# Gated cross-attention with a mixture of experts on one core: another turn table, and two small products split into quadrants of 32 rows

## The chip, the cores and the metric

The kernel runs on one core of a Trainium2 chip. A core has a matrix engine (TensorE, in the profile PE, with its weight loads as PEld), a vector engine (VectorE, DVE), a scalar engine (ScalarE, ACT), a general engine (GpSimd, POOL) and a queue engine (SyncE, SP), each with its own instruction stream in program order, and 16 DMA engines. The metric is device time in microseconds for one execution; less is better.

## The reference, cut to what matters

64 batches of 128 tokens with 128 features, a context of 77 tokens a batch, 16 heads of 8, and 8 experts of which each token takes 2. All float32.

```python
x = x + tanh(g_xattn) * attention(layernorm(x), ctx, mask)     # 16 heads, 77 keys, then Wo
n = layernorm(x)
gate = softmax(n @ Wg)                     # 8 experts
topk_scores, topk_idx = top_k(gate, 2)
topk_scores /= topk_scores.sum(-1) + 1e-8
fused = (n @ W11) * sigmoid(n @ W11) * (n @ W12)    # per expert, inner width 256
x = x + tanh(g_ffn) * sum_k topk_scores[k] * (fused @ W2)[topk_idx[k]]
```

The kernel computes each token only for the two experts that it takes: rows are scattered to the region of their expert in DRAM, worked off in tiles of 128 rows, and scattered back.

## The kernel before, in words

**Groups and turns.** Four batches are a group, so there are 16 groups of 512 tokens. The attention runs in 64 turns, one for each batch. In turn i, PE computes the score products of batch i (`scores`, L865), transposes the scores of batch i-1 (`turn`, L887), mixes values for batch i-2 (`mix`, L919, 24 short products of 32 columns for each of two halves), makes the value blocks of batch i+2 (`values`, L838 and L850, 12 very short products) and transposes what is left of i-1 (`turn_last`, L900). DVE takes maxima of the scores and subtracts them (L874, L877), ACT takes exponentials. The scores have one PSUM buffer, so a turn's scores wait for the subtraction of the turn before.

**The turn table.** All else is done by groups, in steps. The table `AT` gives each step a turn, counted from the group's first, and PRE or POST, before or after that turn's own work. Group g does step s in turn 4g + AT[s]. So in any turn steps of several groups meet, and four turns are a period in which one group's worth of each step is done. Within one place steps run by group number. A POST step of a turn is issued just before a PRE step of the next. The order on PE, ACT, DVE and POOL is the program's order; SP's is planned.

**The steps that the change touches.** Loads (`loads`), statistics, shift and rows of the first layernorm (`stats_a*`, `shift_a`, `rows_a*`), the context's masks on POOL (`sel_0` to `sel_2`), the queries (`queries_t`, `queries`), then after the attention the quotients (`quotients`), the output product (`project`, L589), the sum (`residual`, L595), and the second layernorm (`stats_f*`, `shift_f`, `rows_t`). Then comes the routing: `logits` (four products of a batch's 128 tokens with the gate weights, 8 columns, L642), `less_max`, `gates_exp`, `gates` and `experts` on DVE (two best of eight, L661 to L685), `counts` on POOL (running counts of each expert, L693 and L697), `places` (two products, L705 and L708: how many rows stand ahead of each token), `places_in` on DVE (the row in DRAM, L713 to L722), and eight scatters a group, `dispatch00` to `dispatch31` (batch, choice): each a memset and an indirect DMA on POOL (L726, L727).

**Two parts.** Groups 0 to 11 are part 0, groups 12 to 15 part 1. When the last group of a part has been counted, `tiles_count`, `tiles_ends`, `tiles_list`, `tiles_turn` and `tiles_keep` make the part's list of tiles, and `bounds0` to `bounds3` have SP write padding behind each expert's rows. In other groups these steps are empty.

**The second half.** After the turns, 142 tiles go through PE (`turned` L1034, `up` L1044, `flip` L1059, `down` L1067), ACT and DVE, and POOL scatters each result (L1075, L1076). Steps of the last groups that had no turn left (`rest`) are dealt out one a tile, in the table's order, during part 0's tiles. A part's row loads (L1030) wait for all of its scatters and paddings. At the end the results are fetched, added and stored.

**PSUM.** All products but scores and values take one of three slots in a ring (`product`); a product waits for the readers of the one three before it.

Of the kernel before, what the change touches and what calls it, by code (L numbers as in the profile page):

```python
# [21 lines left out]
G = 4  # L22
# [3 lines left out]
PRE, POST = 0, 1  # L26
# [11 lines left out]
def tile_gated_xattn_moe(  # L38
# [17 lines left out]
    nc = tc.nc  # L56
    B, S, D = x.shape
    M, CD = context.shape[1:]
    E, _, I = W11.shape
    P = 128  # L60
# [26 lines left out]
    def part_of(g):  # L87
        return parts[g >= SPLIT]
# [22 lines left out]
    gates = const.tile([P, 2], F32, name="gates")  # L111
# [4 lines left out]
    wg = wts.tile([D, E], F32, name="wg")  # L116
# [12 lines left out]
    def load_expert(k):  # L129
# [48 lines left out]
    earlier = const.tile([P, P], F32, name="earlier")  # L178
    nc.gpsimd.memset(earlier, 1.0)
    nc.gpsimd.affine_select(  # L180
        earlier, earlier, pattern=[[1, P]], compare_op=ALU.is_gt, fill=0.0,
        base=0, channel_multiplier=-1,
    )
    ones = const.tile([P, P], F32, name="ones")
# [32 lines left out]
    for q in range(NQ):  # L217
        for k in range(2):
            r = 32 * q + 16 * k
# [89 lines left out]
    with ExitStack() as ph:  # L309
# [77 lines left out]
        def product(shape, n):  # L387
            return ring[0].tile(shape, F32, tag="pr", name=n)

        def transposed(src, n):  # L390
# [10 lines left out]


        AT = {
            "loads": (-15, PRE),
            "stats_a0": (-14, PRE),
            "sel_0": (-14, PRE),
            "stats_a1": (-10, PRE),
            "sel_1": (-13, PRE),
            "shift_a": (-9, POST),
            "sel_2": (-11, POST),  # L410
            "context_t": (-7, POST),
            "rows_a0": (-9, POST),
            "rows_a1": (-8, PRE),
            "keys": (-4, POST),
            "queries_t": (-7, POST),
            "queries": (-5, PRE),
            "inverses": (6, PRE),
            "quotients": (6, POST),
            "project": (7, POST),
            "residual": (7, POST),  # L420
            "stats_f0": (8, POST),
            "stats_f1": (9, PRE),
            "shift_f": (10, PRE),
            "rows_f0": (10, PRE),
            "rows_f1": (11, PRE),
            "rows_f2": (11, PRE),
            "rows_t": (11, POST),
            "logits": (13, PRE),
            "less_max": (13, PRE),
            "gates_exp": (14, PRE),  # L430
            "gates": (15, PRE),
            "experts": (15, PRE),
            "counts": (15, PRE),
            "places": (17, PRE),
            "places_in": (17, PRE),
            "tiles_count": (16, PRE),
            "tiles_ends": (16, PRE),
            "tiles_list": (17, PRE),
            "tiles_turn": (17, POST),
            "tiles_keep": (18, PRE),  # L440
            "bounds0": (18, PRE),
            "bounds1": (18, PRE),
            "bounds2": (18, PRE),
            "bounds3": (20, PRE),
            "dispatch00": (17, POST),
            "dispatch01": (17, POST),
            "dispatch10": (18, PRE),
            "dispatch11": (18, POST),
            "dispatch20": (19, PRE),
            "dispatch21": (19, POST),  # L450
            "dispatch30": (19, POST),
            "dispatch31": (20, POST),
        }
        TURN = {}

# [2 lines left out]
        def step(name):  # L458
            def add(f):
                STEP[name] = f  # L460
                TURN.setdefault(AT[name], []).append(name)
                return f

            return add
# [173 lines left out]
        @step("logits")  # L638
        def logits(gr, g):
            gr.pg = product(ge, f"pg_{g}")  # L640
            for b in range(G):
                nc.tensor.matmul(  # L642
                    gr.pg[:, b, :], gr.xT[:, b * S : (b + 1) * S], wg, start=True, stop=True
                )

        @step("less_max")
        def less_max(gr, g):
# [54 lines left out]
        @step("places")  # L702
        def places(gr, g):
            gr.pp = product(ge, f"pp_{g}")
            nc.tensor.matmul(gr.pp, earlier, gr.both, start=True, stop=False)  # L705
            pt = part_of(g)
            i = (g - pt.g0) * G
            nc.tensor.matmul(gr.pp, ones, pt.run[:, i : i + G], start=False, stop=True)  # L708

        @step("places_in")  # L710
        def places_in(gr, g):
# [267 lines left out]
        for i in range(NBT + 2):  # L979
# [8 lines left out]
            if 0 <= i - 2 < NBT:  # L988
                g, b = divmod(i - 2, G)
# [143 lines left out]
        for g in range(SPLIT):  # L1133
            for j, f in enumerate((combine(0), combine(1), store)):
                k = t0 + 3 + (TOPK * g + min(j, 1)) * n1 // (TOPK * SPLIT)
# [52 lines left out]
```

## Time and profile before

| | us |
|---|---|
| median of 3 runs | 690.18 (686.12 to 691.53) |
| profiled execution: its time | 691.94 |
| its span, first to last instruction | 690.2 |
| PE busy | 622.8 |
| POOL busy | 444.5 |
| ACT busy | 438.1 |
| DVE busy | 431.4 |
| first score product, last score product | 20.1, 379.0 |
| first and last product of the tiles | 389.4, 671.3 |

The mean granted clock of TensorE is 0.957. The page gives busy times by engine and, in 40 equal slices, by time; below that stand the chain of work that ended last and the costliest groups of instructions, each with the idle time of its engine before it and what ended it ("issue": nothing that the profile shows). In tables of windows the columns are the window, its length, busy time and number of instructions of PE, PEld, DVE, ACT and POOL, the clock granted to TensorE, the DMA engines' busy share and GB/s. In a timeline they are start, duration, engine, line, operation, and in brackets the idle time before it. A float32 product is two records on PE.

### The profile page before, as it was taken

The numbers are of one execution on the slowest core, as the hardware profiler recorded it, in microseconds if no ns is written. First come the engines' busy times: TensorE is split into PE (matmuls) and PEld (weight loads), VectorE is DVE, ScalarE is ACT, GpSimd is POOL, SyncE is SP. The second block draws the span as 40 slices with busy tenths as digits, with TensorE's granted clock in tenths as the row PEclk, the third lists the DMA queues.
The fourth block names the chain that finished last, engine by engine and source line by source line (L and its number), as shares of the span: only waits on it lengthen the run. The fifth ranks groups of instructions, "written<-read, shape, count | busy, mean of one in ns | idle before, by whom it ended". The sixth has DMA issues, their size and how long they took to land.

```text
span 690.2 us, 21362 instructions
## 1 busy us (share of the span) xinstructions
PE 622.8 (90%) x7703; PEld 450.6 (65%) x7703; DVE 431.4 (63%) x1296; ACT 438.1 (63%) x1184; POOL 444.5 (64%) x771
## 2 busy tenths in 40 slices
PE   4799999999999999999997899999987999999980
PEld 3577877777777877777774666656554556556560
DVE  4758799788787878786788544443343433346642
ACT  3698888677767867786764555576463445545450
POOL 4411125576576657666376458888888888888782
PEclk9999999999989999999999899999998999999995
DMA  4493000111111100010012242232322331458825
GB/s 106 124 287 86 16 15 29 38 31 35 29 35 34 33 26 26 22 31 30 18 31 69 68 100 63 73 82 63 83 77 67 92 82 57 104 189 242 246 83 182
DMA packets 64510, 53.55 MB, mean 78 GB/s; under 512 B 14131, under 2 KB 58235, under 8 KB 64408
## 3 DMA queue, kind: packets, MB, share of 16 engines
q1 hardware_dynamic: 46952, 30.78, 17.1%
q0 software_dynamic: 8640, 17.06, 7.3%
q10 hardware_dynamic: 8816, 4.36, 2.2%
q8 instruction: 63, 1.03, 0.7%
q14 instruction: 39, 0.32, 0.2%
HBM read 28.88 MB, written 24.20 MB: 77 GB/s over the span
## 4 chain that ended last, share of the span: by engine, by line
PE 62%; POOL 14%; issue 9%; DVE 5%; ACT 5%; DMA 3%; SPq 1%; POOLq 1%; another core or an unknown queue 0%; DVEq 0%; ACTq 0%
PE po L919 12%; PE pu L1044 9%; POOL yb L1076 9%; PE tp L887 9%; PE sc L865 6%; PE pot L1067 4%; POOL spare_w L1075 3%; PE tl L900 3%; PE pq L566 2%; PE phh L1059 2%; PE py L589 2%; PE pg L642 2%; PE pv L850 2%; PE pc L528 2%; PE ptt L1034 2%
## 5 line engine op out<-in xcount | busy, mean ns | idle before, releaser
L727 POOL DMA_INDIRECT xg<-rows,dest x128 | 129.0, 1007 | 70.0 <-DVE gm L649 44.4
L1076 POOL DMA_INDIRECT yb<-y,xt x142 | 139.6, 983 | 34.7 <-issue 16.0
L1044 PE MATMUL pu<-wx,xTt 128*128 x284 | 155.1, 629 | 6.6 <-issue 5.6
L1052 DVE TENSOR_TENSOR ht<-sgt,pu 128x256 f32<-128x256 f32 x142 | 59.9, 422 | 113.8 <-ACT sgt L1050 56.9
L1050 ACT ACTIVATE sgt<-pu 128x256 f32<-128x256 f32 x142 | 54.6, 384 | 92.8 <-PE pu L1044 51.6
L874 DVE TENSOR_REDUCE mx<-sc 128x16 f32<-128x1232 f32 x64 | 91.8, 1434 | 31.8 <-PE sc L865 24.6
L1059 PEld LDWEIGHTS phh<-ident,ht 128*128 128x128 f32 x284 | 39.5, 142 | 81.5 <-issue 66.3
L892 ACT ACTIVATE pT<-tp,drop 128x512 f32<-128x512 f32 x128 | 81.3, 680 | 12.6 <-PE tp L887 11.8
L1067 PE MATMUL pot<-wx,hTt 128*128 x568 | 87.0, 276 | 0.0
L887 PEld LDWEIGHTS tp<-ident,pe 128*128 128x128 f32 x512 | 60.5, 151 | 31.5 <-issue 9.2
L877 DVE TENSOR_TENSOR pe<-sc,mx 128x1024 f32<-128x1024 f32 x64 | 78.4, 1225 | 2.2
L887 PE MATMUL tp<-ident,pe 128*128 128x128 f32 x512 | 77.3, 298 | 1.3 <-ACT kb L555 0.6
L1067 PEld LDWEIGHTS pot<-wx,hTt 128*128 128x128 f32 x568 | 75.0, 192 | 0.2 <-ACT y L1073 0.2
L1073 ACT ACTIVATE y<-pot,xt 128x128 f32<-128x128 f32 x142 | 52.6, 370 | 24.0 <-PE ptt L1034 9.1
L1036 DVE COPY xTt<-ptt 128x128 f32<-128x128 f32 x142 | 41.4, 291 | 39.0 <-PE phh L1059 14.7
L370 POOL TENSOR_TENSOR rs_a<-rs_a,live 128x4 f32<-128x4 f32 x15 | 3.0, 201 | 89.7 <-ACT rs_a L367 81.8
L865 PE MATMUL sc<-kb,qT 32*128 32x308 f32 x512 | 56.8, 512 | 3.5 <-ACT kb L555 1.8
L919 PE MATMUL po<-pT,va 128*32 128x128 f32 x1536 | 57.2, 284 | 3.0 <-issue 2.3
L919 PE MATMUL po<-pT,own 128*32 128x128 f32 x1536 | 58.6, 277 | 1.4 <-issue 1.4
L1059 PE MATMUL phh<-ident,ht 128*128 128x128 f32 x284 | 55.0, 276 | 3.4 <-ACT hTt L1061 3.2
L1061 ACT COPY hTt<-phh 128x256 f32<-128x256 f32 x142 | 52.4, 369 | 8.6 <-PE ptt L1034 6.0
L1044 PEld LDWEIGHTS pu<-wx,xTt 128*128 128x128 f32 x284 | 43.9, 195 | 17.8 <-issue 16.4
(169 smaller groups left out, 1140.9 us busy)
## 6 DMA issues: line engine op xcount, KB each, us to landing
xt<-xg SPq DMA_DIRECT2D x142, 66.0 KB
ys<-yb SPq DMA_DIRECT2D x16, 512.0 KB
x<-in_x_dram SPq DMA_DIRECT2D x15, 256.0 KB
out_dram<-x ACTq DMA_DIRECT2D x15, 256.0 KB
yb<-y,xt POOLq DMA_INDIRECT x142
wx<-in_L_ffn_W_dram SPq DMA_DIRECT2D x2, 1024.0 KB
xg<-rows,dest POOLq DMA_INDIRECT x128
xg<-empty SPq DMA_DIRECT2D x30, 66.0 KB
```

The costliest lines, as they stand in the source:

```text
L727: i = nc.gpsimd.indirect_dma_start(out=part_of(g).xg[:, :], out_offset=bass.IndirectOffsetOnAxis(ap=gr.dest[:, k, b : b + 1], axis=0), in_ ...
L865: nc.tensor.matmul(sc[:, q, :W], gr.qT[r, b * S : (b + 1) * S], gr.kb[r, b].rearrange("p h j -> p (h j)"), start=True, stop=True,)
L874: nc.vector.tensor_reduce(mx[:, :, :, 0], sv, AX.X, ALU.max)
L877: nc.vector.tensor_tensor(dst[:, :, :, : j1 - j0], sv[:, :, :, j0:j1], mx.to_broadcast([P, NQ, HQ, j1 - j0]), ALU.subtract,)
L887: nc.tensor.transpose(tp[:, u, :], pe[:, q + u // 2, 2 * (u % 2) : 2 * (u % 2) + 2].rearrange("p h j -> p (h j)"), ident,)
L892: nc.scalar.activation(pT[:, 2 * q : 2 * q + 4], tp, AF.Exp, bias=drop[:, 0, i : i + 1], scale=scale)
L919: nc.tensor.matmul(po[32 * q : 32 * q + 32, v, :], w, pT[:, 2 * q + c if c < 2 else 8 + q // 2, :], start=(c == 0), stop=(c == 2),)
L1044: nc.tensor.matmul(pu.rearrange("p j i -> p (j i)"), ti.xT, wxf[:, bass.ds(ti.e, 2 * I)], start=True, stop=True,)
L1052: nc.vector.tensor_tensor(ti.h.rearrange("p c i -> p (c i)"), sg, pu[:, 1], ALU.mult)
L1059: nc.tensor.transpose(pt[:, c], ti.h[:, c], ident)
L1067: nc.tensor.matmul(po, ti.hT[:, c], wxf[:, bass.ds(ti.e + w, D)], start=(c == 0), stop=(c == NC - 1),)
L1076: i = nc.gpsimd.indirect_dma_start(out=ti.pt.yb[:, :], out_offset=bass.IndirectOffsetOnAxis(ap=ti.x[:, D : D + 1].bitcast(I32), axis=0), i ...
```

## The change

The table `AT` gets other turns. Most of the routing comes sooner by a half to two turns: the gates' exponential, `gates`, `experts`, `places` (from before turn 17 to after turn 15), the tile list and seven of eight scatters by more than one turn. `quotients`, `project` and `residual` come one turn later, `queries_t` one sooner, `bounds3` two later. And `logits` and `places` are split: in place of one product with 128 rows of result there are four with 32 rows each, which take 32 columns of the stationary operand each. `logits` has 16 products instead of 4, `places` 8 instead of 2. Nothing else changes.

```diff
-            "loads": (-15, PRE),
+            "loads": (-16, POST),
             "stats_a0": (-14, PRE),
             "sel_0": (-14, PRE),
             "stats_a1": (-10, PRE),
-            "sel_1": (-13, PRE),
-            "shift_a": (-9, POST),
-            "sel_2": (-11, POST),
+            "sel_1": (-11, POST),
+            "shift_a": (-10, POST),
+            "sel_2": (-10, POST),
             "context_t": (-7, POST),
-            "rows_a0": (-9, POST),
+            "rows_a0": (-8, PRE),
             "rows_a1": (-8, PRE),
             "keys": (-4, POST),
-            "queries_t": (-7, POST),
+            "queries_t": (-8, POST),
             "queries": (-5, PRE),
             "inverses": (6, PRE),
-            "quotients": (6, POST),
-            "project": (7, POST),
-            "residual": (7, POST),
+            "quotients": (7, POST),
+            "project": (8, POST),
+            "residual": (8, POST),
             "stats_f0": (8, POST),
             "stats_f1": (9, PRE),
-            "shift_f": (10, PRE),
+            "shift_f": (9, POST),
...
-            "rows_t": (11, POST),
+            "rows_t": (12, PRE),
             "logits": (13, PRE),
             "less_max": (13, PRE),
-            "gates_exp": (14, PRE),
-            "gates": (15, PRE),
-            "experts": (15, PRE),
+            "gates_exp": (13, PRE),
+            "gates": (14, POST),
+            "experts": (14, POST),
             "counts": (15, PRE),
-            "places": (17, PRE),
-            "places_in": (17, PRE),
-            "tiles_count": (16, PRE),
-            "tiles_ends": (16, PRE),
-            "tiles_list": (17, PRE),
-            "tiles_turn": (17, POST),
-            "tiles_keep": (18, PRE),
-            "bounds0": (18, PRE),
-            "bounds1": (18, PRE),
-            "bounds2": (18, PRE),
-            "bounds3": (20, PRE),
-            "dispatch00": (17, POST),
-            "dispatch01": (17, POST),
-            "dispatch10": (18, PRE),
-            "dispatch11": (18, POST),
-            "dispatch20": (19, PRE),
-            "dispatch21": (19, POST),
-            "dispatch30": (19, POST),
-            "dispatch31": (20, POST),
+            "places": (15, POST),
+            "places_in": (15, POST),
+            "tiles_count": (15, POST),
+            "tiles_ends": (15, POST),
+            "tiles_list": (16, PRE),
+            "tiles_turn": (16, POST),
+            "tiles_keep": (16, POST),
+            "bounds0": (15, POST),
+            "bounds1": (17, POST),
+            "bounds2": (17, POST),
+            "bounds3": (22, PRE),
+            "dispatch00": (15, POST),
+            "dispatch01": (16, PRE),
+            "dispatch10": (16, POST),
+            "dispatch11": (16, POST),
+            "dispatch20": (16, POST),
+            "dispatch21": (16, POST),
+            "dispatch30": (18, PRE),
+            "dispatch31": (19, POST),
...
             for b in range(G):
-                nc.tensor.matmul(
-                    gr.pg[:, b, :], gr.xT[:, b * S : (b + 1) * S], wg, start=True, stop=True
-                )
+                for r in range(0, P, 32):
+                    nc.tensor.matmul(
+                        gr.pg[r : r + 32, b, :], gr.xT[:, b * S + r : b * S + r + 32], wg,
+                        start=True, stop=True,
+                    )
...
             gr.pp = product(ge, f"pp_{g}")
-            nc.tensor.matmul(gr.pp, earlier, gr.both, start=True, stop=False)
             pt = part_of(g)
             i = (g - pt.g0) * G
-            nc.tensor.matmul(gr.pp, ones, pt.run[:, i : i + G], start=False, stop=True)
+            for k, (w, of) in enumerate(((earlier, gr.both), (ones, pt.run[:, i : i + G]))):
+                for r in range(0, P, 32):
+                    nc.tensor.matmul(
+                        gr.pp[r : r + 32], w[:, r : r + 32], of, start=(k == 0), stop=(k == 1)
+                    )
```

## The prediction

> **What bounds the kernel now.** I read the page first: which engine is full, and where. PE is busy 90% of the span and the chain that ended last lies on it for 62%.
>
> ```profile
> PE 622.8 (90%) x7703; PEld 450.6 (65%) x7703; DVE 431.4 (63%) x1296; ACT 438.1 (63%) x1184; POOL 444.5 (64%) x771
> ...
> PEclk9999999999989999999999899999998999999995
> ```
>
> The clock row has dents at slices 12, 23 and 31; it rounds shorter ones away. The table of windows, cut at starts of score products four turns (one period, one group of batches) apart or a multiple of it, shows them all.
>
> ```profile
> 129.03:226.49 97.46, 92.86 (x1602) 73.83 (x1601) 76.72 (x232) 71.78 (x189) 61.49 (x112) 0.91 0.12 33
> 226.49:248.73 22.24, 21.36 (x402) 17.11 (x401) 19.04 (x58) 17.71 (x48) 15.39 (x28) 1.00 0.11 33
> 248.73:297.82 49.09, 47.08 (x801) 37.46 (x800) 38.34 (x116) 35.94 (x95) 30.75 (x56) 0.90 0.08 25
> ```
>
> The first row is four periods (24.4 us each, clock 0.91), the last two (24.5, 0.90), the middle one period at full clock (22.2). Same work: a period that meets the half clock is 2.2 us longer, and there are six such periods (and one more dent at 320 us). PE is busy 94 to 96% of these rows, so PE sets the pace. Where the half clock comes from:
>
> ```profile
> 241.72:245.36 3.64, 3.58 (x76) 2.77 (x75) 3.50 (x5) 2.73 (x6) 3.14 (x6) 1.00 0.11 37
> 245.36:248.78 3.42, 2.71 (x33) 2.41 (x33) 1.66 (x9) 2.35 (x8) 0.98 (x2) 1.00 0.08 25
> 248.78:252.19 3.41, 3.41 (x23) 2.24 (x26) 3.16 (x9) 1.85 (x6) 2.66 (x4) 0.50 0.07 22
> ```
>
> A 3.4 us window with 33 PE products instead of some 80 is followed by 3.4 us at 0.50. Two things thin that window. One: `values` (L838, L850) is a burst of 24 short products, and where it meets a scatter (L727 on POOL) it halts.
>
> ```profile
> 239.69 0.30 PE L838 MATMUL pv<-wv,cT 96*32 96x64 f32 x8
> 239.80 0.29 PE L850 MATMUL pv<-wv,czs 96*32 96x16 f32 x16
> ...
> 253.02 1.00 POOL L727 DMA_INDIRECT xg<-rows,dest  x1 [0.16 <-issue]
> ...
> 253.51 0.33 PE L850 MATMUL pv<-wv,czs 96*32 96x16 f32 x10
> ...
> 254.31 0.29 PE L850 MATMUL pv<-wv,czs 96*32 96x16 f32 x6 [0.47 <-issue]
> ```
>
> Undisturbed the burst runs through; under a scatter it stops for 0.47 us with nothing awaited. In the timeline of 125 to 300 us this happens about twice (1.1 us) in the turn before `logits` and once (0.5 us) in the one after, nearly every period. Two: right behind come `places` and `logits`, which move 32 and 8 columns.
>
> ```profile
> L642 PE MATMUL pg<-wg,xT_f 128*128 128x8 f32 x128 | 17.3, 262 | 0.0
> L642 PEld LDWEIGHTS pg<-wg,xT_f 128*128 128x128 f32 x128 | 16.3, 198 | 0.2
> ...
> L708 PE MATMUL pp<-run,ones 128*128 128x32 f32 x32 | 6.2, 276 | 0.0
> L705 PEld LDWEIGHTS pp<-both,earlier 128*128 128x128 f32 x32 | 5.7, 190 | 1.5
> ```
>
> `logits` is 8 records in 1.0 us, 0.125 us each: the pace of 128-column weight loads. `places` is 4 in 0.63 us.
>
> **Part 1: the quadrants.** `logits` becomes 32 records of 32 columns, `places` 16. Nearest row: the burst above, 24 records in 0.42 us, 17.5 ns each (the L919 products: 24 in 0.57 to 0.68). So 32 x 17.5 = 0.56 us for 1.0, and 16 x 17.5 = 0.28 for 0.63: 0.79 us a group. Against it stands the Trainium skill: "TensorE: Matmul & The Clock Gate", section LDWEIGHTS, prices a load by its columns at P/1.2 ns, so four quarters cost what the whole cost: 32 x 27 = 0.85, 16 x 27 = 0.43, saving 0.35; and "TensorEngine Tiling", Key Properties, says that a change of tiling mode drains the engine. The trace contradicts the load price (17.5 ns) and prices the drain: weight loads idle 0.17 us at the step from the 128-column transposes to L919. Two switches more a group, some 0.3 us, is the charge. Saving: 0.79 less 0.3, about 0.5; ends 0 and 0.8. PE takes 28 instructions more each for loads and products; if bursts of them meet scatters, that is rival C.
>
> **Part 2: the table.** A step at (k, POST) stands beside one at (k+1, PRE); call that boundary k+1. By boundary, modulo 4: PE had transposed rows and `project` at 0, keys, `places`, `logits` at 1, context and query transposes at 2, queries at 3. Now: `places` and transposed rows at 0 (before 1.6 us, now 0.35 + 0.5); `project` (1.06), keys (0.5), query transposes (0.5), `logits` (0.6) at 1; context (0.8) at 2; queries (1.1) at 3. No PE work goes; it moves. What the move does: `places` leaves the thin window and `project` with 8 products of 128 columns enters it, so that window gets roughly 25 products more of 32 to 128 columns (estimate from these counts).
>
> Scatters (1.52 us each with their memset, L726 + L727 + 0.16) stood at 18, 18, 18, 19, 19, 20, 20, 21; now 16, 16, 17 four times, 18, 20. The first waits for `places_in` on DVE, which follows the previous turn's subtraction by 1.1 us. Laid out from a score start S at boundary 0: scatters at S+1.2, 2.7, 4.2, 5.8, 7.3, 8.8, the eighth after `sel_1` at 11.2. PE runs L919 and `values` at S+1.8 to 3.5: one scatter meets them, one halt (0.5 us) where two were. In the next turn `values` falls near S+10.2 to 10.6, between the scatters: none for one. So about 0.5 us of halts for 1.6. Ends: 0 and 2.7 (all bursts hit).
>
> Waits added: `places` follows `counts` by one turn, not two. Behind it on PE wait transposed rows and the next scores. `counts` can start when `took` is written, some 1.3 us into `gates`; with 0.27 + 1.04 us on POOL it ends about 1 us before PE arrives (POOL has `sel_0` and `sel_2` ahead of it, two scatters no longer). `project` to `residual` to the PSUM slot of `logits`: the add ends 0.9 us after `project`, while keys and transposes run 1.0 us: free. Query transposes put 0.6 us of copy on ACT in the keys' boundary, where the second score transpose may wait 0.1 us. DVE then nearly sets the pace. Its turn is 3.0 us (L874 1.43, L877 1.23 and 0.37), and its work at boundaries 2 and 3 is 1.8 (shift, statistics) and 2.2 (`gates`, `experts`, shift). From the scores of boundary 1, whose maxima start 1.35 us late (statistics behind `logits`): 1.35 + 3.0 + 1.8 + 3.0 + 2.2 + 3.0 + 0.1 = 14.45 to the scores of boundary 0; from there PE, 4.3 (0.8 + 1.02 + 1.23 + 0.42 + 0.3, with one halt) and 2.9 for boundary 1 and its switches. So a period at full clock is an estimated 21.7 us, 0.5 below the 22.2.
>
> SP: `loads` moves half a turn; `bounds` issue only for groups 11 and 15, and the trace has all eight of a part in one row (8.2 us at 361.65) whatever their turns; the row loads behind them wait for scatters until 380.3 and are used from 389. Free. At group 11 the tile list (2.6 us) joins `tiles_ends`, `places_in`, `quotients` at boundary 60: PE loses an estimated 2.4 us there; now it loses 2.3 before 368.79, where the list stands alone with the same effect. Zero.
>
> FFN: four scatters fewer are left for it, 6 us of POOL; hidden, since from 628 us on every result scatter starts within 1.4 us of its product, and before that its lag (8 tiles at most, of 20 buffers) stops no product: PE sets the pace. But the last `places` comes two tiles after `counts`, where `tiles_count` came four later and already waited:
>
> ```profile
> PEld pcount L758 <- POOL run L697: 3.8, 1, 3.8
> ```
>
> POOL gets there 6.1 us sooner (four scatters of 1.52 fewer ahead), PE four tiles of 1.93: from 3.6 us the wait becomes an estimated 5.2, +1.6; three `places` and two `logits` save 1.2. About zero, +1 with the drain of the last turns.
>
> **The clock.** "TensorE: Matmul & The Clock Gate", the table under "Why this matters for your kernels", asks only that PE have no idle gap over some 3 us. In the row of 245.36 no gap is over 0.7 us, and the half clock came. By the rule there is no clock to win: 14 groups x 0.5 less 1, -6 and 684. By the row a fuller window keeps it. I follow the row, but leave two of the periods dented.
>
> **Sum**, on the profiled execution (span 690.2, its time 691.94): six periods from 24.4 to 21.7 and one from 22.2, -16.7; two still dented, +4.4; the dent at 320 gone, -1.5; six other groups' products, -3.2; end and FFN, +1. Total -16: 676 of 691.94. That execution lay 1.8 above the median of 690.18, within the runs' own spread of 686.12 to 691.53; I leave it at **676**. Own range 667 to 684 (no dent, no halt, the row's 0.8 us a group; or five dents left).
>
> **Rivals.**
> A, forecast: the thin window fills, 676. Chance 0.52.
> B, the clock stays: `logits` now ends boundary 1 and its window is just as thin. Only the products' 6 us are left, or half where DVE is level: 684 to 687, say 686. For it: the period of 226.49 kept its clock with the same thin stretch, so where the windows fall decides too, and the trace doesn't show the threshold. Chance 0.22.
> C, slower: PE at `places` waits for `counts`. In the trace `counts` ended at 240.06 and the turn's last transpose at 240.5: a margin of half a microsecond, though with two scatters ahead of it on POOL that are gone. It decides once POOL, or `gates` before it, is over 1 us later than laid out; then PE idles 1.5 us, the idle keeps every half clock, and the scores behind are late by as much: 13 x 1.5, less 5 of products, +3 in the FFN: 707. Against it: POOL idles 3 to 5 us a period before `rs_a`. Chance 0.2.
> D, the lap is given back: DVE, now level with PE, takes 22.5 us a period. -1.9 x 6 + 0.3 + 4.4 - 3.2 + 1: -9, 682. Chance 0.06, beside A.
>
> **Numbers.** Within 1% (683.3 to 697.1) is about what a measurement of this kernel can tell from no change. Faster: A nearly whole, D: 0.56. Same: B, slim parts of A and C: 0.23. Slower: 0.21. The range takes A's lower end and half of C: 665 to 704.
>
> **What would show it.** Right: granted clock near 0.98 or more between 129 and 298, periods of about 21.7; the records of `logits` near 20 ns apart; `place` no longer waiting for `pp` (14.3 us now); attention's last score 12 us or more before 379. Wrong: PE or PEld rows at `pp` waiting for POOL `run` (C); dents as many as now (B); DVE `pls` releasing scores every turn (D).

## The result, and the profile after

The change takes 723.56 us (median of 4 runs, 719.73 to 728.63) where the kernel before takes 690.86 (686.12 to 692.58): 1.049 of it, 95% interval 1.040 to 1.058. It is slower; 676 was forecast. The profiled execution took 719.73 us (span 718.0) against 691.94.

First the page of the changed kernel: busy time, the clock row, and the chain that ended last by engine.

```profile
PE 626.2 (87%) x8279; PEld 445.3 (62%) x8279; DVE 431.0 (60%) x1296; ACT 441.7 (62%) x1184; POOL 444.2 (62%) x771
...
PEclk9999998999999989999889889999999999999995
...
PE 75%; DVE 9%; issue 6%; ACT 3%; another core or an unknown queue 3%; POOL 2%; DMA 2%; SPq 0%; DVEq 0%; POOLq 0%; ACTq 0%
```

PE's busy time rose by 3.4 us, the rest of the span, in which it is idle, from 67.4 us to 91.8: most of the 28 us between the two spans are waits. "Another core or an unknown queue" is 3% of a chain in a kernel that has one core: waits whose end the profile can't put down to anything. The last score product starts at 407.44 us for 379.04, and the stretch from there to the end is 310.5 us for 311.1: the whole loss lies in the attention. Now the table of windows, cut as before at starts of score products (four periods, one, two; columns as before):

```profile
136.86:237.75 100.89, 87.61 (x1754) 67.24 (x1745) 76.88 (x235) 72.12 (x189) 60.63 (x113) 0.97 0.11 33
237.75:263.12 25.37, 22.95 (x445) 17.42 (x437) 19.14 (x58) 17.96 (x48) 14.27 (x28) 0.91 0.10 30
263.12:315.39 52.27, 46.84 (x873) 35.70 (x872) 38.06 (x115) 36.39 (x96) 30.57 (x57) 0.91 0.08 23
```

A period is 25.2 to 26.1 us. In the first row the clock is 0.97, better than the 0.91 of before, and yet each period is 0.9 us longer. PE is busy 87% of it, no longer 95%. So in this row it isn't the clock: PE waits. Split by turn, from the scores of turn 16 to those of 63, the turns that begin in phase 0 (turn number a multiple of 4; boundary 0 to boundary 1) took 114.9 us together where they took 79.9; those of phase 1 took 1.0 less, of phase 2 6.1 less, of phase 3 1.4 more. It is one turn in four: 9.6 us on average where 6.7 was and 7.2 was laid out.

The two products themselves did what they were to do (groups by form, mean ns of one after the bar):

```profile
L643 PE MATMUL pg<-wg,xT_f 128*32 128x8 f32 x512 | 8.4, 187 | 3.3 <-DVE x L595 1.2 <-ACT va L861 1.2 <-ACT pT L910 0.7
L711 PE MATMUL pp<-both,earlier 128*32 128x32 f32 x128 | 4.9, 205 | 0.9 <-issue 0.2
L711 PE MATMUL pp<-run,ones 128*32 128x32 f32 x128 | 4.5, 200 | 0.6 <-POOL run L699 0.6
```

`logits` is 8.4 us of busy time for 17.3. And no row of `pp` waits long for POOL: rival C isn't it.

### The profile page after: what moved, and what is told of

Its sections match the earlier page's. It is cut to its first block, busy times and chain, and to the rows that moved or that the text cites. A ratio compares the mean times of both kernels' runs of the same rounds, so it can differ in the third digit from the quotient of the medians.

```text
span 718.0 us, 22543 instructions
## 1 busy us (share of the span) xinstructions
PE 626.2 (87%) x8279; PEld 445.3 (62%) x8279; DVE 431.0 (60%) x1296; ACT 441.7 (62%) x1184; POOL 444.2 (62%) x771
## 4 chain that ended last, share of the span: by engine, by line
PE 75%; DVE 9%; issue 6%; ACT 3%; another core or an unknown queue 3%; POOL 2%; DMA 2%; SPq 0%; DVEq 0%; POOLq 0%; ACTq 0%
PE pu L1049 17%; PE po L924 12%; PE tp L892 9%; PE pot L1072 8%; PE sc L870 7%; PE phh L1064 4%; PE tl L905 3%; PE ptt L1039 3%; DVE mx L879 2%; PE pq L566 2%; DVE pe L882 2%; PE pk L549 2%; PE pv L855 2%; PE py L589 1%
## 5 line engine op out<-in xcount | busy, mean ns | idle before, releaser
L1049 PE MATMUL pu<-wx,xTt 128*128 x284 | 153.1, 621 | 5.5 <-issue 4.3
L732 POOL DMA_INDIRECT xg<-rows,dest x128 | 127.6, 997 | 43.4 <-DVE dest L727 22.3
L892 PE MATMUL tp<-ident,pe 128*128 128x128 f32 x512 | 79.0, 302 | 5.7 <-DVE gp L653 4.8
L870 PE MATMUL sc<-kb,qT 32*128 32x308 f32 x512 | 60.4, 515 | 3.0 <-ACT kb L555 1.8
L924 PE MATMUL po<-pT,va 128*32 128x128 f32 x1536 | 60.6, 293 | 0.5 <-issue 0.5
L924 PE MATMUL po<-pT,own 128*32 128x128 f32 x1536 | 56.7, 278 | 1.0 <-issue 1.0
L1080 POOL MEMSET spare_w<- 128x320 f32 (+1 forms) x142 | 53.9, 380 | 0.1
```

The lines of the kernel that those rows point to most:

```text
L732: i = nc.gpsimd.indirect_dma_start(out=part_of(g).xg[:, :], out_offset=bass.IndirectOffsetOnAxis(ap=gr.dest[:, k, b : b + 1], axis=0), in_ ...
L870: nc.tensor.matmul(sc[:, q, :W], gr.qT[r, b * S : (b + 1) * S], gr.kb[r, b].rearrange("p h j -> p (h j)"), start=True, stop=True,)
L892: nc.tensor.transpose(tp[:, u, :], pe[:, q + u // 2, 2 * (u % 2) : 2 * (u % 2) + 2].rearrange("p h j -> p (h j)"), ident,)
L924: nc.tensor.matmul(po[32 * q : 32 * q + 32, v, :], w, pT[:, 2 * q + c if c < 2 else 8 + q // 2, :], start=(c == 0), stop=(c == 2),)
L1049: nc.tensor.matmul(pu.rearrange("p j i -> p (j i)"), ti.xT, wxf[:, bass.ds(ti.e, 2 * I)], start=True, stop=True,)
```

## Where the time went

The timeline of one such turn of the changed kernel (scores of turn 36 at 227.56 us; start, length, engine, line, operation, the idle time before it):

```profile
230.01 0.97 POOL L732 DMA_INDIRECT xg<-rows,dest  x1 [0.17 <-issue]
...
231.32 0.33 PE L855 MATMUL pv<-wv,czs 96*32 96x16 f32 x13 [0.35 <-issue]
231.52 0.97 POOL L732 DMA_INDIRECT xg<-rows,dest  x1 [0.17 <-issue]
...
232.28 1.30 PE L589 MATMUL py<-wo,aT 128*128 128x128 f32 x8
...
232.90 0.27 ACT L931 COPY os<-po 128x128 f32<-128x128 f32 x1 [1.96 <-PE tl L905]
...
233.03 0.97 POOL L732 DMA_INDIRECT xg<-rows,dest  x1 [0.17 <-issue]
...
234.54 0.96 POOL L732 DMA_INDIRECT xg<-rows,dest  x1 [0.17 <-issue]
...
235.88 0.48 ACT L861 COPY va<-pv 128x384 f32<-128x384 f32 x1 [2.53 <-remote]
236.02 0.69 DVE L595 TENSOR_TENSOR x<-x,py 128x512 f32<-128x512 f32 x1 [4.50 <-remote]
236.05 0.97 POOL L732 DMA_INDIRECT xg<-rows,dest  x1 [0.16 <-issue]
...
236.79 0.42 PEld L394 LDWEIGHTS pt_a<-ident,xn 128*128 128x128 f32 x4 [3.09 <-ACT va L861]
```

The records of `pv` end at 231.65 us, those of `py` at 233.58. ACT's copy of `pv` starts at 235.88, DVE's addition of `py` at 236.02. Nothing else was awaited: both wait only on PE's semaphore, and that counts once at 232.88, then three times between 235.86 and 236.00. In between POOL runs one scatter after another. PE's results were late by 4.2 and 2.4 us, and then PE itself stood still for 3.1 us at `pt_a`, whose slot in the ring of three is that of `tl`, read by ACT behind the late copy. The waits of the attention show that this is the rule (in total, times, longest; of the changed kernel, then of the kernel before):

```profile
DVE x L595 <- remote: 38.4, 9, 5.1
...
ACT os L931 <- PE tl L905: 28.1, 15, 6.0
POOL xg L732 <- DVE dest L727: 17.0, 10, 1.8
...
ACT va L861 <- PE pk L549: 15.9, 9, 2.5
PEld pt_a L394 <- ACT va L861: 14.2, 6, 3.1
...
PE pt_a L394 <- ACT va L861: 11.3, 6, 2.6
...
PE pv L855 <- issue: 5.7, 14, 0.5
...
PE pt_a L394 <- ACT pT L910: 5.4, 3, 1.9
```

```profile
PE pv L850 <- issue: 7.8, 19, 0.5
```

In the twelve turns of phase 0 between the scores of turns 16 and 63, PE's idle time grew from 6.8 us to 29.3. The halts inside the `values` bursts have hardly a part in that: 6.3 us before, 6.8 after (and in the turns of phase 1 they fell from 2.3 us to nothing). 18.1 us are `pt_a`, the query transposes waiting for their slot, a wait that the kernel before doesn't have, and 3.1 us are `logits` behind the same late readers. PE is also busy 12.6 us longer in these turns, mostly by the work that the table moved there.

I call a result late when its reader still waits after the product is done. I added up, for each instruction of ACT and DVE that reads a product, the idle time that lies after the end of that product's own records, where it is over 0.8 us: 48 cases and 86 us between 60 and 400 us of the changed kernel, 19 cases and 22 us before. Before, the same thing was there, small enough that I read it as the halts of `values` alone.

**Theory 1:** scatters that run on POOL one behind another hold back PE, its instructions and its results; the change puts six of them in a row into the turn of phase 0. **Theory 2:** the moved attention steps (`project`, `residual`, query transposes in the boundary of keys and `logits`) wait on one another in the ring, with or without scatters. Later came **theory 3**, halts are a property of the chip, and **theory 4**, the table loses by waits of its own without any halt.

## The experiments

Kernels sent together ran on one chip and share their runs of the kernel before. That kernel took 704 us with e1 to e4, 654 with e5 to e8, 705 with f1 to f4, 691 with g1 to g4, 653 with h1 and h2. These differences between sessions are themselves a finding; ratios are to the kernel before of the same session. A session in which results are late is called one with halts.

### The halves of the change, and the scatters alone

e1, the quadrants in the table of before (`logits` and `places` as in the change's diff, nothing else):

> The turn table of before with logits and places as products by quadrants: the second half of the change alone. Theory 1 (the loss is in the table: indirect DMAs issued one behind another on POOL hold back PE's results) and theory 2 (the loss is in the table too, but in the attention steps moved to the boundary of keys) agree here: 16 groups save about 0.6 us of logits and 0.3 of places each, less what is hidden: 682 to 689 for 690.9. If quadrants cost PE something (drains, instruction supply), it is above 692.

Measured: 694.67 us, 0.984 (0.980 to 0.989). 9.6 us for 16 groups, 0.6 a group, a little more than expected (0.987 to 0.997).

e2, the new table with whole products:

> The new turn table with whole products: the other half of the change alone. Both theories put the loss here: 723.6 plus what the quadrants save, 725 to 735. Below 715 would mean that table and quadrants hurt only together.

Measured: 760.15 us, 1.079 (1.074 to 1.084). The table makes the loss, and more of it than either theory had given it (1.05 to 1.06).

e3, in the changed kernel:

```diff
-            "dispatch00": (15, POST), "dispatch01": (16, PRE), "dispatch10": (16, POST), "dispatch11": (16, POST),
-            "dispatch20": (16, POST), "dispatch21": (16, POST), "dispatch30": (18, PRE), "dispatch31": (19, POST),
+            "dispatch00": (17, POST), "dispatch01": (17, POST), "dispatch10": (18, PRE), "dispatch11": (18, POST),
+            "dispatch20": (19, PRE), "dispatch21": (19, POST), "dispatch30": (19, POST), "dispatch31": (20, POST),
```

> The changed kernel with the eight dispatch rows alone back at their turns of before (17 POST to 20 POST); gates, places, projections and the rest stay moved. Theory 1: the four scatters at (16, POST) with the two before them make a run of six in front of project and residual, and PE's results reach ACT and DVE 2 to 4 us late in it; apart from them the turn of phase 0 to 1 falls from 8.5 to 10 us back to about 7, so 690 to 700. Theory 2 (project, query transposes and logits in one boundary wait in a ring over three PSUM slots, with or without scatters): 715 to 724.

Measured: 721.17 us, 1.023 (1.017 to 1.030). Between the two theories. e4, the same rows at (15, POST), (16, PRE), (16, POST), (17, PRE) and so on to (19, PRE):

> The changed kernel with two scatters at each of four boundaries (15 POST and 16 PRE, 16 POST and 17 PRE, 17 POST and 18 PRE, 18 POST and 19 PRE), none in a run of more than two. Theory 1: no result of PE waits for more than about 2 us; the phase 0 to 1 turn falls to some 7 us; 690 to 702. Theory 2: 715 to 724.

Measured: 740.88 us, 1.050 (1.045 to 1.055), no better. A miss for theory 1 as I had put it, but the traces say why: the turn in the table isn't the time at which POOL scatters. POOL runs through its own order until an instruction of it waits. The waits of e3:

```profile
POOL rs_a L370 <- ACT rs_a L367: 59.6, 8, 9.1
DVE x L595 <- PE py L589: 35.0, 9, 6.2
```

POOL stands idle 7 us a period in front of `rs_a`, because it has run all scatters before. In the kernel before, the first scatter of a group had to wait for `dest` in the turn of phase 1 (3.0 us of idle POOL there, by the timeline), and that broke the run: three scatters met the turn of phase 0. In e3 `dest` comes a turn and a half sooner, nothing stops POOL, and turn 36 again has five scatters, and a `values` burst of 2.98 us, where 1.82 was before and 0.41 is undisturbed. In e4 it has five in a row as well: its `values` bursts are stretched by only 0.6 us in a turn of phase 0, but 35 results are late, by 83 us together, and the turn takes 10.1 us on average.

### Gate chain and attention rows apart

e5, table of before, quadrants, and the change's rows from `gates_exp` to `dispatch31`; e6 its complement, the change's rows for the attention with those of before for the gate chain.

> The table of before and the quadrant products, with the rows of the gate chain (gates_exp to dispatch31) as in the change; projections, query transposes and statistics stay at their old turns. Theory 1 (what decides is where POOL runs scatters one behind another; it stops only where an instruction of its waits: at the first scatter for dest, at rs_a, at both): dest now comes in the turn of phase 0 and six scatters run through to the boundary of keys: ratio to the kernel before 1.02 to 1.05, for the 0.984 that the quadrants alone gave. Theory 2 (project, transposes and logits in one boundary): 0.98 to 0.995.

> The complement: the quadrant products and the moved attention rows (loads, sel, shift, rows_a, queries_t, quotients, project, residual, shift_f, rows_t), with the gate chain and the scatters at the turns of before. Theory 1: dest still comes at boundary 1 and breaks the run of scatters, but project and residual now stand at the boundary where PE's results come late: 0.98 to 1.00. Theory 2: the loss stays, 1.02 to 1.06.

Measured: 652.01 us, 0.998 (0.997 to 0.999), and 660.30, 1.012 (1.008 to 1.015). Both theories missed both. Something else had changed: beside these four the kernel before took 653.75 us. In the profiles of e5 to e8 no result is over 0.8 us late and no `values` burst in the periods is stretched. Why e6 loses 1.2% without either stays open. e7 and e8 make each scatter wait for the newest `pe`:

```diff
+                if cur[0] is not None:
+                    nc.gpsimd.tensor_copy(spare_w[:, 0:1], cur[0][:, 0, 0, 0:1])
                 nc.gpsimd.memset(spare_w, 0.0)
```

> The changed kernel, its scatters at two a boundary from (16, POST), and each made to wait: POOL first copies one element of the latest pe, so that it can't run ahead of DVE by more than a turn; 64 small copies more on POOL. Theory 1: no run longer than two or three, after 3.2 us of a turn, so `values` and `project` meet few of them: the turn of phase 0 to 1 falls under 8 us and the ratio to 0.97 to 1.01. Theory 2: the turn stays at 9 us or more, ratio 1.03 to 1.05.

> The table of before with quadrant products, the scatters paced in the same way, two a boundary from (17, POST). Theory 1: in the quadrants kernel alone three scatters still run through the turn of phase 0 and stretch its `values` burst to 1.9 us; paced they miss it: 0.96 to 0.98, below the 0.984 of the quadrants alone. Theory 2 says nothing of it: 0.98 to 0.99. If the copies make POOL late, above 0.99.

Measured: 679.67 us, 1.040 (1.037 to 1.043), and 659.22, 1.008 (1.005 to 1.012). Without halts the pacing can save nothing, and it makes POOL late. (e7's ratio lies where theory 2 had it, but its turn of phase 0 takes 6.9 us, not 9.) The waits of e7:

```profile
POOL spare_w L734 <- DVE pe L886: 47.0, 22, 4.2
...
PEld pp L711 <- POOL both L695: 12.7, 10, 1.5
PE pp L711 <- POOL both L695: 10.4, 9, 1.2
```

That is rival C: PE at `places` waits for `counts`, here because POOL was held back. It makes up 10.4 us of e7's loss of 26; the second half is longer too (315.3 us, 306.6 in e5).

The repeat, with the change, the kernel before for its profile, and the two halves that had been measured in different sessions:

> The changed kernel as it is, once more. In the last four kernels' profiles, taken on another chip, PE nowhere stops under a scatter and no result of it reaches ACT or DVE late, and the kernel before takes 654 us there, not 690 to 704. Theory 3 (the halts under scatters are a property of the chip that a kernel runs on, and the change's loss is made of halts): where the kernel before takes some 654 us, the change takes 640 to 655, where it takes 690 or more, 1.04 to 1.06 of it. Theory 4 (the new table loses without halts as well, by waits that it adds itself): 1.01 to 1.05 at 654 us too.

> The kernel before as it is, for its profile on the same chip as the change's. At 654 us, by theory 3: no `values` burst over 0.6 us and no result that waits over 0.8 us, periods of 21 to 22 us; at 690 or more: bursts and waits as in the first profile.

> The quadrants alone, once more. Without halts, by theories 3 and 4 alike: the products' 0.5 to 0.8 us a group, 7 to 12 of 654, 0.982 to 0.99; with halts 0.984 as measured.

> The table of before with quadrants and the gate chain moved, once more: 0.998 on the chip without halts. Where the chip halts (690 us or more for the kernel before), theory 1 says 1.02 to 1.05, because six scatters run through the turns of phase 0 and 1.

Measured, with halts: the change 762.68 us, 1.082 (1.075 to 1.089); the kernel before 706.88 with 26 late results, 36 us; the quadrants 694.92, 0.988 (0.981 to 0.996); the gate chain 754.19, 1.071 (1.064 to 1.078). The change and the gate chain lose more than theories 3 and 1 had said (1.04 to 1.06 and 1.02 to 1.05). The gate chain leaves the attention steps where they were and loses all the same, so theory 2, which gave it 0.98 to 0.995, falls. It also makes the clearest pair of the study: e5 and f4 are the same kernel, on two chips in two sessions. The same turn 36 in both, first the timeline of PE in f4:

```profile
241.22 0.30 PE L843 MATMUL pv<-wv,cT 96*32 96x64 f32 x7
...
242.62 0.22 PE L855 MATMUL pv<-wv,czs 96*32 96x16 f32 x2 [0.51 <-issue]
243.37 0.27 PE L855 MATMUL pv<-wv,czs 96*32 96x16 f32 x5 [0.53 <-issue]
244.12 0.28 PE L855 MATMUL pv<-wv,czs 96*32 96x16 f32 x4 [0.49 <-issue]
...
247.15 0.52 PE L643 MATMUL pg<-wg,xT_f 128*32 128x8 f32 x20 [0.45 <-issue]
```

and in e5:

```profile
207.55 0.30 PE L843 MATMUL pv<-wv,cT 96*32 96x64 f32 x8
207.66 0.29 PE L855 MATMUL pv<-wv,czs 96*32 96x16 f32 x16
...
208.92 0.44 PE L643 MATMUL pg<-wg,xT_f 128*32 128x8 f32 x32
```

POOL runs scatters 1.52 us apart through both. In f4 PE gets two to five products through, stops for half a microsecond, and goes on; in e5 the whole burst runs. The turn and the period after it, f4 then e5:

```profile
238.14:247.59 9.45, 7.03 (x125) 4.78 (x124) 4.45 (x9) 3.54 (x9) 8.53 (x13) 0.84 0.14 45
247.59:274.19 26.60, 23.36 (x440) 17.85 (x437) 19.18 (x58) 17.90 (x48) 15.20 (x29) 0.88 0.09 27
```

```profile
204.46:209.29 4.83, 4.83 (x125) 3.65 (x124) 4.45 (x9) 3.93 (x11) 4.27 (x7) 1.00 0.14 45
209.29:230.01 20.72, 20.22 (x447) 15.71 (x437) 18.95 (x58) 17.66 (x48) 15.33 (x29) 1.00 0.12 35
```

Same instructions, 9.45 us and 4.83; the clock is 0.84 and 0.88 in f4, full in e5.

### Without indirect DMAs

g1 and g2 are the change and the kernel before with each scatter replaced (rows are not sorted by expert):

```diff
-                i = nc.gpsimd.indirect_dma_start(out=part_of(g).xg[:, :], ...
+                r = pt.cap * (TOPK * b + k) + P * (g - pt.g0)
+                i = nc.sync.dma_start(out=pt.xg[r : r + P, :], in_=gr.rows[:, b, k, :])
```

> The changed kernel, each scatter replaced by a plain DMA of the same 128 rows that SP issues to a fixed place (so rows are not sorted by expert; POOL keeps the small memsets; one filling DMA a group is added). PE, DVE and ACT do the same work, POOL issues no indirect DMA in the attention. Theory 1 (indirect DMAs halt PE): on a chip that halts, periods of 26 to 29 us fall to 20 to 21.5 and the last score from 407 to 433 us to 340 to 350. Theory 4 (the table itself loses): periods stay over 23 us.

> The same replacement in the kernel before. Theory 1: no `values` burst over 0.6 us, periods of 21 to 22 us, the last score at 350 to 360 us; the plain change is then level with it or up to 2% faster, since nothing but the products is left between them. Theory 4: the plain change is 2% or more slower than this.

Measured: 639.21 us (638.97 to 639.42) and 646.34 (644.00 to 647.67), in a session in which the kernel before took 690.77 and the two other kernels have late results (17 and 10 between 60 and 400 us). The periods and the last scores (346.4 and 357.4 us) lie where theory 1 had them. One period of each, windows:

```profile
215.30:235.53 20.23, 19.89 (x446) 15.73 (x437) 18.82 (x60) 17.71 (x48) 7.48 (x20) 1.00 0.13 36
```

```profile
222.04:243.06 21.02, 20.82 (x402) 16.70 (x401) 19.35 (x59) 17.57 (x48) 6.89 (x20) 1.00 0.13 34
```

No late result in either. The totals also hold a second half on other rows, so I compare turn 16 to turn 63: 237.5 us and 247.8, where the traces of the first pair, with halts, have 307.4 for the change and 278.0 for the kernel before. That the indirect DMAs make the halts is shown for the kernel before, since it and g2 ran on one chip in one session, beside the two kernels with late results; the change with its scatters wasn't run in that session. The replacement takes away the instruction on POOL and its DMA queue together, so which of them halts PE isn't separated; the memsets stayed on POOL and halt nothing. And without the scatters the new table with its quadrants is the faster one (1.1% in the totals). g3 and g4 repeat e6 and e8 where halts occur:

> Quadrants and moved attention rows with the scatters of before, once more (1.0115 on the chip without halts). On a chip that halts, by theory 1: dest still breaks the run of scatters at boundary 1, but one run of three or four meets `values` of phase 0 and the results of `project` behind it: 1.00 to 1.03. If the gate chain alone makes the loss, 0.98 to 1.00.

> The quadrants with paced scatters, once more (1.0085 on the chip without halts). On a chip that halts, theory 1: runs of at most three, most of them after `values`: 0.97 to 1.00. If a scatter costs its halts wherever it stands, 1.00 to 1.03.

Measured: 686.52 and 677.29 us, 0.994 and 0.980 by medians. Six of the seven runs of the kernel before took 688.77 to 692.12, one 677.88; beside that one the ratios are 1.013 and 0.999, so I give no interval, and what the attention rows cost isn't decided. It is less than the 8.5% of the gate chain (f4 against f3). Paced, the quadrants have 10 late results, 10 us, where f3 had 17 and 24 us in its session: fewer halts, as theory 1 said; that the pacing saves time beside the quadrants alone (0.984 and 0.988 in other sessions) isn't shown.

### The change once more, and scatters further apart

h2 puts three memsets ahead of each scatter:

```diff
-                nc.gpsimd.memset(spare_w, 0.0)
+                for _ in range(3):
+                    nc.gpsimd.memset(spare_w, 0.0)
```

> The changed kernel a third time, as the measure for the next one. Where the kernel before takes 675 us or more: 1.04 to 1.09 of it. Where it takes some 654 us (no halts): 0.98 to 1.00 if what is left without halts is the gain that the two plain kernels show (0.989), 1.01 to 1.04 if the scatters' order on POOL costs without halts as well.

> The changed kernel with three memsets of 0.38 us before each scatter instead of one: a scatter every 2.3 us or so instead of 1.5. If the halts belong to each scatter (PE stops from some 0.1 to 0.6 and 0.7 to 1.3 us after its start), fewer of them fall into the turn of phase 0, and the ratio falls by 0.02 to 0.05 below that of the change. If the halts grow with the memsets, or POOL's lateness is what is paid for, it rises by 0.02 or more.

Measured: the kernel before 653.46 us, no halts this time, on the same chip as g1 to g4. Theory 3 falls: it is not the chip. The change: 646.59 us, 0.989 (0.987 to 0.990): 1.1% less than the kernel before, where with halts it took 5 to 8% more. Lines of its page, and its windows, cut at the scores of turns 21, 37 and 41 as above:

```profile
PE 584.8 (90%) x8279; PEld 424.4 (66%) x8279; DVE 427.3 (66%) x1296; ACT 439.2 (68%) x1184; POOL 443.6 (69%) x771
...
PEclk9999999999999999999999799899987999999995
```

```profile
128.83:210.27 81.44, 79.55 (x1754) 62.92 (x1745) 76.03 (x234) 71.77 (x189) 60.43 (x113) 1.00 0.14 40
210.27:230.69 20.42, 19.88 (x446) 15.73 (x437) 19.01 (x60) 17.98 (x48) 15.13 (x29) 1.00 0.13 39
```

A period is 20.4 us at full clock. Theory 4 falls too, for the change as a whole; the table alone and the quadrants alone weren't run without halts. h2 took 699.60 us, 1.070 (1.068 to 1.072). Whether a halt is paid for each scatter stays open, since none occurred. Its loss, POOL's lateness as its expectation named it, shows in its waits:

```profile
PEld pp L711 <- POOL both L695: 11.9, 9, 3.0
```

POOL, 8 x 0.76 us later a period, holds up `places`, and PE behind it: rival C again. In the second half `places` waits once more, for 15.0 us; that half takes 327.1 us where h1 needs 304.6.

## Why the prediction was wrong

**The step that failed** is a wait that "Waits added" put at nothing: "`project` to `residual` to the PSUM slot of `logits`: the add ends 0.9 us after `project`, while keys and transposes run 1.0 us: free." While scatters follow one another on POOL, ACT and DVE get PE's results late. The add doesn't end 0.9 us after `project`, since `x` waits 4.3 us a time (38.4 over 9); and the query transposes, in the same boundary, stand still for 18.1 us over the twelve turns of phase 0, because readers of their slot were late (26.3 us in f1). These turns took 2.9 us more each (35.0 us over 12) where the layout had 7.2 us, half a microsecond over the 6.7 of before. Without halts (h1) `pt_a` waits nowhere in the attention, and such a turn takes 6.1 us.

The halts of "Part 2" were not what failed. The layout of the scatters came nearly as forecast: S+1.2, 2.7, 4.2, 5.8, 7.3, 8.8 there, S+0.7, 2.4, 4.0, 5.5, 7.0, 8.5 in the trace of turn 36. The `values` burst of phase 0 is stretched by 0.95 us (0.5 forecast), that of phase 1 not at all, as forecast; between turns 16 and 63 the stretching is 12.8 us in all, for 17.1 before. So the sign was right, and 0.4 us a period were saved of 1.1. But the price of a scatter was counted in bursts alone, so that "2.7 (all bursts hit)" was no outer end. A row that said so was in the trace of before:

```profile
244.91 0.27 PE L919 MATMUL po<-pT,own 128*32 128x128 f32 x1
...
244.99 0.97 POOL L727 DMA_INDIRECT xg<-rows,dest  x1 [0.16 <-issue]
...
246.50 0.27 ACT L926 COPY os<-po 128x128 f32<-128x128 f32 x1 [1.07 <-PE po L919]
```

ACT's `os` starts 1.3 us after `po` is done, with a scatter in between, eight times between 126 and 296 us; in e5, without halts, it is never over 0.4 us there.

**The quadrants:** 0.5 us a group forecast, 0.6 measured (e1), but that the two agree is in part luck. f2 and f3 ran in one session. From turn 20 to turn 39, at full clock, the turn of phase 0 falls from 6.9 us to 6.4, as the products should make it, but that of phase 1 rises from 5.3 to 5.8: its `values` burst is stretched more (0.89 us a turn over the attention, 0.64 in f2). A period is 22.1 us for 22.3. Nearly all of f3's gain in the attention, 11.6 us, comes in the five periods after that, where f2 has five windows of half clock and f3 one; these four make at most some 7 us (an estimate: half of 4 x 3.4), and the rest wasn't traced.

The products themselves came out as the trace had them: undisturbed, 32 records of `logits` take 0.44 us where 0.56 was reckoned and 1.0 was. The load price that the prediction took from the Trainium skill ("TensorE: Matmul & The Clock Gate", section LDWEIGHTS; 27 ns for 32 columns) would have given an estimated saving of 0.35 us a group; the trace has 32 weight loads of `logits` in 0.35 us, 11 ns each.

**Table and quadrants without halts:** the sign was right. 0.5 us a period at full clock was forecast for both together, and the plain pair shows 0.8; the table's own share wasn't measured. The period itself is 20.4 us (h1), not 21.7, since the kernel before, too, takes 21.0 once its scatters are gone (g2).

**The clock:** 16 windows of 3.4 us at half clock between 108 and 402 us, where the kernel before has 11 from 129 to 399. The five more are at most some 8.5 us of the loss (an estimate: half of 5 x 3.4). The forecast that fewer halts in `values` bring back the clock isn't borne out as a rule. In e5, g1 and h1, without halts, the attention has no half clock from 87 us to 355 us; but g2 has two such windows between 200 and 290 us and h2 eight between 147 and 318 us, also without any late result, while e1 and f3, with halts, have none from 35 us to 313 and 333 us.

**The waits and the rest:** `places` doesn't wait for `counts` in the attention of h1. Its one long wait, 6.9 us, is the last one in the second half, where an estimated 5.2 was forecast. So C's margin was judged about right; e7 and h2 show its price once POOL is late. DVE's turns of phases 2 and 3 came as laid out (4.8 and 5.3 us; 4.7 and 5.3 in the trace). The second half is level, 310.5 us for 311.1. Of rival B the sign came, as many dents as before or more, but not the time; D didn't come. The missing rival was one in which the scatters cost more than before, since the table puts six of them in a row into one turn.

Of the forecast -16 us against 691.94 (0.977), the chip gives -7 of 653 (0.989) without halts, and +33 to +58 with them. Of the versions run, the quadrants alone are the safest where halts occur (0.984 and 0.988), and beat the change there; without halts they were not run.

## What to carry to other kernels

Where halts occur, a scatter on POOL is not priced by POOL's time, nor by the short PE instructions that lie under it: count the readers of PE's results under a run of scatters, too, and look in the trace of before for results that are fetched late. A step's turn in an order written by hand is not its time: on an in-order engine, the instruction that waits sets the pace of all behind it, and feeding it earlier lets everything behind it run into one heap. And a few per cent of a kernel that scatters while PE works should be measured in more than one session before they are believed.

## What was not expected of the hardware

While indirect DMAs followed each other 1.52 us apart, PE's semaphore reported products long after the end of their records (4.2 us in the turn shown), and bursts of PE instructions stopped twice in each scatter's cycle. In the stretched bursts of the kernel before, of the changed kernel, of e3 and of f4 they started again 0.6 us and 1.3 to 1.4 us after a scatter's start. The trace doesn't say whether PE worked later than its records (their ends are modelled) or only reported later.

It occurs in some sessions (medians of 691 to 705 us for the kernel before) and not in others (653 and 654), and for one chip both are on record; within a session nearly all executions agree. It isn't confined to the attention: in the second half, which scatters its results, f2 has 38 late results (51 us) and takes 324.3 us, e5 has 4 (5 us) and takes 306.6. A scatter takes 0.97 us and its memset 0.38 in both kinds. What decides between them no run here shows.
